# Another order within a step, a two-tile band, and the inner norm on one engine, in a two-layer banded kernel

## The chip, the cores and the metric

The kernel runs on one core of one Trainium2 chip. The metric is device time in microseconds (us), the median over runs. In the profile PE is TensorE's matmul queue and PEld its weight loads, DVE is VectorE, ACT is ScalarE, POOL is GpSimd and SP the engine that issues most DMAs.

## What is computed

x is [512, 512, 64] in float32. Two layers of the same form follow each other, x = x + f(gn(x)), where gn normalizes each pair of channels over the whole image. With m the mask product, L = 512, H = 128 and a window of 4, f is

```
xn    = ln(x)                                  # over the 64 channels
left  = (xn @ Wl + bl) * m * sigmoid(xn @ Wlg + blg)
right = (xn @ Wr + br) * m * sigmoid(xn @ Wrg + brg)
gate  = sigmoid(xn @ Wog + bog)
out[i, j, h] = sum over d in -4..4 of left[i + d, i, h] * right[i + d, j, h]
f     = (ln(out) * gate) @ Wo + bo
```

All is float32. Only a band of `left` is needed: row i + d of column i. For each h the sum over d is a small banded matrix (rows by rows) times the rows of `right`.

## The kernel before, in words

**Tiling.** `row_blocks` cuts the 512 rows into nine overlapping blocks of 64 rows (56 of them new, 60 at the ends). The image's left half of columns lies on partitions 0 to 63 and its right half on 64 to 127, e = 0 and 1. A block is two chunks of 128 columns a half, a chunk is 16 units (`NU`) of 8 columns (`JU`). So a layer has 18 chunks and 288 units. `layer` (line 748) runs steps t; a step carries one unit through projection and, 30 steps later (`LAG`), one `Out` through its end. The two layers run one after the other.

**A step**, for unit t and output t:

- `affine` and `inner_stats` prepare z of later units; `inner_norm` (437) and `inner_norm_v` (443) subtract the mean and scale, for the unit two steps ahead. GpSimd does six of eight columns in two instructions, VectorE the other two (`ZV`, 27) in two.
- `transposed` (450) turns z of the next unit on TensorE, `kept` (469) copies it from PSUM to `zT` on ScalarE, with a third part that repeats the first 64 columns, and stores it to `later` for the output's gates.
- `right` (514) projects the unit in two halves q = 0 and JQ = 4 through `crossed` (499): 8 matmuls a half, each with 64 rows, 128 columns of weights and 128 moving columns. `right_gate` (517) is the sigmoid on ScalarE, `right_end` (521) the product on VectorE into `RO`, a buffer that holds the right values of a chunk and later its outputs.
- `mix` (575) is the band: for 8 of the 128 h's it multiplies the banded left operand `A` with `RO`, 16 matmuls of 64 by 64 with 128 moving columns. The h's are split into two groups; the second group's results are written on the other half of the partitions (the "crossed" columns), so that all four 64x64 tiles of TensorE's array are used in turn. The result goes back from PSUM to `RO`, half by a ScalarE copy, half by a VectorE copy. A chunk has 16 mixes, spread over the first ten of 16 steps as 2, 1, 2, 2, 1, 2, 1, 2, 2, 1.
- `out_stats` (601) takes the statistics of `RO` on VectorE, `solve` (607) makes the scales every fourth step (a few small VectorE instructions, then a chain of small ones on GpSimd), `norm` (640) applies them on ScalarE into `on` (one buffer), 8 instructions a step in two groups of four.
- `gates` (653) and `gated` (666) make the output gate, `turned` (677) turns `on`, `times_gate` (690) multiplies both on VectorE into `ZH`. A step later `end` (713) multiplies by Wo, and `ended` (727) adds the residual, which `biased` (707) has prepared on GpSimd, and stores it. In layer 0 `sums` (736) collects the statistics for layer 1 on TensorE.

**The left operand.** In five early steps of a layer (3, 5, 7, 9, 11) `left` (528) projects the band of left into `L9`, a part of `RO`, and writes it to DRAM (`left_of`) when a row of nine is complete: 4 x 9 transfers a layer in pieces of 72 bytes. `take_left` (559) fetches 16 h's (`HA`) as `A` in four transfers with pieces of 512 bytes, [h, row, 2], into one of three buffers (`NA`).

**What sets the order.** Each engine runs its instructions in the order in which the program issues them (`InOrder`, 366, keeps the program's order). The order is that of the calls in lines 844 to 921, so moving a call moves its instructions on each engine's queue. PSUM has eight banks: `two_banks` (132) hands out two pairs in turn, to both right halves, the transposes and the mixes, in the order of the calls; each waits until the use two before it has been read. Four single banks go round among `gates`, `turned` and `end`.

Of the kernel before, what the change touches and what calls it, by code (L numbers as in the profile page):

```python
# [16 lines left out]
P = 128  # L17
# [9 lines left out]
ZV = 2  # L27
# [53 lines left out]
def tile_two_banded_layers(  # L81
# [28 lines left out]
    span = 2 * (S + 2 * WIN)  # L110
    size = S * H // 2 * span
# [325 lines left out]
    def inner_norm(u: Unit):  # L437
        n = ZV if u.at > NU else 0
        m = last(u.mean.rearrange("p k t -> p (k t)")[:, n:], D)
        en.gpsimd.tensor_tensor(u.z[:, n:], u.z[:, n:], m, ALU.subtract)  # L440
        en.gpsimd.tensor_tensor(u.z[:, n:], u.z[:, n:], last(u.rs[:, n:], D), ALU.mult)

    def inner_norm_v(u: Unit):
        for j in range(ZV if u.at > NU else 0):
            en.vector.tensor_scalar(
                u.z[:, j], u.z[:, j], u.mean[:, j // 2, j % 2 : j % 2 + 1], u.rs[:, j : j + 1],
                ALU.subtract, ALU.mult,
            )
# [20 lines left out]
    def kept(u: Unit):  # L469
        u.t = ztp.tile([P, JU // 2, P + S], F32, tag="zT", name="zT")  # L470
        to = u.t.rearrange("c k (n p) -> c n k p", n=3)
        for n, pt in enumerate(u.pt):
            en.scalar.activation(
                to[:, n : n + pt.shape[1]], pt.rearrange("c n (k p) -> c n k p", p=S),
                AF.Identity, bias=1.0,
            )
        if u.near is None:
            en.scalar.activation(
                to[:, 2], u.pt[0][:, 0].rearrange("c (k p) -> c k p", p=S), AF.Identity, bias=1.0
            )  # L480
            en.sync.dma_start(later[u.at], u.t[:, :, :P])
# [5 lines left out]
    def projected(u: Unit, q: int, w: bass.AP):  # L487

        pr = two_banks().rearrange("p (e k h) -> p e k h", e=2, k=JQ // 2)
        for k in range(JQ // 2):  # L490
            for e in range(2):
                part = slice(e * D, (e + 1) * D)
                en.tensor.matmul(
                    pr[:, e, k, :], lhsT=u.t[part, q // 2 + k, :P], rhs=w[part],
                    start=True, stop=True,
                )
        return pr

    def crossed(u: Unit, q: int, w: bass.AP):

        pr = two_banks().rearrange("p (e k h) -> p e k h", e=2, k=JQ // 2)
        for k in range(JQ // 2):
            for s in range(2):
                for e in range(2):
                    part = slice(e * D, (e + 1) * D)
                    en.tensor.matmul(
                        pr[:, e, k, :].rearrange("p (g s x) -> p g s x", g=2, s=2)[:, :, s],
                        lhsT=u.t[part, q // 2 + k, s * S : s * S + P],
                        rhs=w[part].rearrange("c (g s x) -> c g s x", g=2, s=2)[:, :, s],
                        start=True, stop=True,  # L510
                    )
        return pr

    def right(u: Unit, q: int, w: dict):
        u.pr[q] = crossed(u, q, w["right"]).rearrange("p e k h -> p (e k) h")
# [12 lines left out]
    def left(u: Unit, q: int, w: dict):  # L528
# [4 lines left out]
        sv = sg.rearrange("p (k e) h -> p e k h", e=2)  # L533
        for e in range(2):
            en.scalar.activation(sv[:, e], pr[:, e, :, H:], AF.Sigmoid)
        near = w["near"][:, n0 : n0 + JQ]
        en.gpsimd.tensor_tensor(sg, sg, last(near, H), ALU.mult)
        for e in range(2):
            en.vector.tensor_tensor(
                L9[:, :, n0 + e : n0 + JQ : 2, :],  # L540
                pr[:, e, :, :H].rearrange("p k (h t) -> p h k t", t=2),
                sv[:, e].rearrange("p k (h t) -> p h k t", t=2), ALU.mult,
            )
        for r in range(JQ):
            if n0 < (r + 1) * NEAR <= n0 + JQ:
                for n, b in enumerate(blocks):
                    q0 = b.s // JQ
                    at = n * size + r * (H // 2 * span + 2)
                    en.sync.dma_start(
                        strided(  # L550
                            left_of, at, (JQ * (H // 2 * span + 2), S // JQ), (span, H // 2),
                            (1, 2 * NEAR),
                        ),
                        L9[q0 : q0 + S // JQ, :, r * NEAR : (r + 1) * NEAR, :].rearrange(
                            "q h k t -> q h (k t)"
                        ),
                    )

    def take_left(n: int, h: int) -> bass.AP:


        A = lp.tile([P, HA // 2, S, 2], F32, tag="A", name="A")
        q = HA // 4
        for e in range(2):
            for s in range(2):
                en.sync.dma_start(
                    A[e * S : (e + 1) * S, s * q : (s + 1) * q].rearrange("p h i t -> p h (i t)"),
                    strided(
                        left_of, n * size + (s * H // 4 + h * q) * span + 2 * WIN,
                        (H // 2 * span, S), (span, q), (1, 2 * S),  # L570
                    ),
                )
        return A

    def mix(c: int, A: bass.AP, h0: int) -> list:


        j0 = c % 2 * (JC - JW)
        q = HB // 4
        R = RO.rearrange("p (s h) j t -> p s h j t", s=2)[:, :, h0 // 4 : h0 // 4 + q, j0 : j0 + JC]  # L580
        L = A.rearrange("p (s h) i t -> p s h i t", s=2)[:, :, h0 % HA // 4 : h0 % HA // 4 + q]
        pb = two_banks()
        ph = pb.rearrange("i (s h t j) -> i s h t j", s=2, h=q, t=2)
        for h in range(q):
            for t in range(2):
                for s in range(2):
                    for e in range(2):
                        part, to = (slice(n * S, (n + 1) * S) for n in (e, e ^ s))
                        en.tensor.matmul(
                            ph[to, s, h, t, :], lhsT=L[part, s, h, :, t], rhs=R[part, s, h, :, t],  # L590
                            start=True, stop=True,
                        )
        return [(R[:, s], ph[:, s].rearrange("i h t j -> i h j t")) for s in range(2)]

# [153 lines left out]
    def layer(src: bass.AP, dst: bass.AP, w: dict, stats: bool, then=None):  # L748
# [60 lines left out]
        for t in range(min(loads), last_t + 3):  # L809
# [34 lines left out]
            if t in lefts:  # L844
                for q in range(0, min(JU, NEAR * JQ - lefts[t].near), JQ):
                    left(lefts[t], q, w)
            if t in outs:
                gates(outs[t], w)
            if t in units:
                right(units[t], 0, w)  # L850
# [6 lines left out]
            if t in outs:  # L857
                gated(outs[t])
            if t in units:
                right_gate(units[t], 0)  # L860
            for v in looking[0:2]:
                out_stats(*v)
            for u in inputs(t + 2):
                inner_norm(u)
            for v in looking[2:5]:
                out_stats(*v)
            for v in todo:
                inner_stats(*v)
            if t in outs:
                turned(outs[t], w)  # L870
            for v in looking[5:]:
                out_stats(*v)
# [6 lines left out]
            if t in units:  # L879
                right_gate(units[t], JQ)  # L880
            if t in outs:
                biased(outs[t], w, stats)
            if t in units:
                right_end(units[t], 0)
# [173 lines left out]
```

## Time and profile before

| | |
|---|---|
| three runs, us | 4828.45, 4837.08, 4837.57; median 4837.08 |
| the profiled execution, us | 4837.08, of which its span 4835.3 |
| mean granted TensorE clock | 0.967 |
| ScalarE `on<-RO,nm,rs` 128x128 (`norm`) | 4608 of 499 ns mean, 1928.5 us busy |
| TensorE `banks<-pack,zT`, 128 columns (`right`) | 18432 of 285 ns mean, 1327.0 us busy |
| TensorE `banks<-RO,A` (`mix`) | 18432 of 281 ns mean, 632.2 us busy |
| VectorE `z<-z,sti,rs` (`inner_norm_v`) | 1084 of 647 ns mean, 657.1 us busy |
| GpSimd `z<-z,sti` and `z<-z,rs`, 128x384 (`inner_norm`) | 542 each, 842 and 838 ns mean |
| ScalarE `zT<-banks` 128x256 (the third part of zT) | 542 of 381 ns mean, 206.6 us busy |
| DMA, share of 16 engines' span | 73.0% on the first queue |

A float32 matmul stands as two instructions (a load and a matmul each), so a mix is 32. Instructions of one group overlap, and the busy time is the time in which at least one ran: it is less than count times mean. In the window lines below, the first numbers are the bounds of the window in us from the span's start and its length, then the busy time of each engine with its number of instructions. In the lines of waits the numbers are total us, how often, and the longest. Line 374 stands for all calls through `InOrder`, so groups are told apart by the names of their tiles: `banks` is a pair of PSUM banks, `bank` a single one.

### The profile page before, as it was taken

To read this page: it belongs to the slowest core of one execution; us is meant where nothing else is said; L and a number is where in the kernel's file an instruction comes from. 1 tells how busy PE (TensorE), PEld (TensorE's weight loads), DVE (VectorE), ACT (ScalarE), POOL (GpSimd) and SP (SyncE) were. 2 spreads that over 40 slices of the span, in tenths; PEclk is the share of its full clock that TensorE was granted. 3 is DMA by queue.
4 is the path that set the end of the run, shared out by engine and by line. 5 is a ranking of instruction groups with operands and counts; after the bars stand their busy time and mean duration, and the time that the engine had idled before them with its cause. 6 is when DMAs were issued, how large, how long until landed. Compare 5 with 4: busy or idle time off the path is not lost.

```text
span 4835.3 us, 193356 instructions
## 1 busy us (share of the span) xinstructions
PE 3858.8 (80%) x76306; PEld 3246.6 (67%) x76306; DVE 4360.2 (90%) x10719; ACT 3745.5 (77%) x8732; POOL 3599.2 (74%) x4739
## 2 busy tenths in 40 slices
PE   1025899999899998999974578888888888888898
PEld 0024677777777777777754467777777777777775
DVE  6954899999999999999966489999999999999997
ACT  0012798889889898889873278888888888888899
POOL 0035888888888888888634588888888888888863
PEclk9986999999999999999997799999999999999999
DMA  7858677777777777777764967777777777777776
GB/s 301 337 177 100 181 209 213 211 213 208 211 209 214 213 211 205 208 210 217 196 169 99 105 179 212 209 214 208 210 211 214 209 212 210 206 215 214 216 202 177
DMA packets 1437653, 983.61 MB, mean 203 GB/s; under 512 B 167202, under 2 KB 1284424, under 8 KB 1432392
## 3 DMA queue, kind: packets, MB, share of 16 engines
q1 hardware_dynamic: 1432064, 969.75, 73.0%
q8 instruction: 600, 9.83, 0.9%
q14 instruction: 309, 2.53, 0.2%
q10 hardware_dynamic: 4680, 1.50, 0.1%
HBM read 658.42 MB, written 312.46 MB: 201 GB/s over the span
## 4 chain that ended last, share of the span: by engine, by line
PE 39%; DVE 30%; DMA 11%; POOL 6%; issue 5%; ACT 5%; SPq 3%; ACTq 0%; DVEq 0%; POOLq 0%
PE banks L374 20%; PE bank L374 19%; DVE RO L374 8%; DVE z L374 6%; DVE ZH L374 5%; ACT on L374 3%; POOL z L374 3%; SPq L374 3%; DVE gn_st L374 3%; DVE sto L374 3%; DMA zg<-later 2%; DVE XR L374 2%; DVE sti L374 2%; DMA mid_x<-XR 1%; POOL rsqrt L374 1%
## 5 line engine op out<-in xcount | busy, mean ns | idle before, releaser
L374 ACT ACTIVATE on<-RO,nm,rs 128x128 f32<-128x128 f32 x4608 | 1928.5, 499 | 16.1 <-PE bank L374 12.7
L374 PEld LDWEIGHTS banks<-pack,zT 64*128 64x128 f32 x18576 | 1251.7, 195 | 562.5 <-DVE RO L374 304.7
L374 PE MATMUL banks<-pack,zT 64*128 64x128 f32 x18576 | 1359.7, 287 | 318.9 <-DVE RO L374 205.3
L374 DVE TENSOR_TENSOR RO<-banks,sg 128x512 f32<-128x512 f32 (+1 forms) x1188 | 753.1, 672 | 242.6 <-ACT sg L374 119.5
L374 ACT ACTIVATE sg<-banks 128x512 f32<-128x512 f32 (+1 forms) x1188 | 666.3, 594 | 280.4 <-PE banks L374 274.1
L374 DVE BATCH_NORM_STATS2 sto<-RO 128x6 f32<-128x256 f32 x2304 | 798.9, 408 | 1.2
L374 DVE SCALAR_TENSOR_TENSOR ZH<-bank,pack,gate 128x448 f32<-128x448 f32 (+1 forms) x1152 | 738.2, 682 | 63.2 <-ACT gate L374 49.8
L374 PE MATMUL bank<-zg,pack 64*128 64x448 f32 (+1 forms) x2304 | 724.9, 595 | 71.4 <-DMA zg<-later 43.4
L374 POOL TENSOR_TENSOR z<-z,gb 128x512 f32<-128x512 f32 x536 | 686.8, 1281 | 42.0
L374 POOL TENSOR_TENSOR z<-z,ga 128x512 f32<-128x512 f32 x536 | 684.7, 1277 | 6.8 <-DMA z<-in_x_dram 4.0
L374 PE MATMUL bank<-pack,ZH 128*64 128x64 f32 x18432 | 665.6, 225 | 5.6 <-ACT gate L374 5.1
L374 PE MATMUL banks<-RO,A 64*64 64x128 f32 x18432 | 632.2, 281 | 37.8 <-DVE RO L374 6.5
L374 DVE TENSOR_SCALAR z<-z,sti,rs 128x64 f32<-128x64 f32 x1084 | 657.1, 647 | 0.0
L374 PEld LDWEIGHTS bank<-pack,ZH 128*64 128x64 f32 x18432 | 585.8, 138 | 46.7 <-ACT gate L374 9.3
L374 PEld LDWEIGHTS banks<-RO,A 64*64 64x64 f32 x18432 | 531.4, 136 | 89.4 <-DVE RO L374 68.7
L374 ACT ACTIVATE zT<-banks 128x512 f32<-128x512 f32 (+1 forms) x1084 | 470.6, 488 | 134.4 <-PE banks L374 120.2
L374 ACT ACTIVATE gate<-bank 128x448 f32<-128x448 f32 (+1 forms) x1152 | 559.9, 539 | 13.0 <-issue 7.1
L374 POOL TENSOR_TENSOR z<-z,rs 128x384 f32<-128x384 f32 (+1 forms) x586 | 508.1, 867 | 45.9
L374 PE MATMUL bank<-ident,on 64*128 64x64 f32 x9216 | 473.6, 227 | 49.3 <-ACT gate L374 39.4
L374 POOL TENSOR_TENSOR z<-z,sti 128x384 f32<-128x384 f32 (+1 forms) x586 | 512.8, 875 | 0.0
L374 POOL TENSOR_TENSOR XR<-XR,pack 120x512 f32<-120x512 f32 (+1 forms) x352 | 417.2, 1188 | 121.3 <-DMA XR<-mid_x 51.5
L374 DVE BATCH_NORM_STATS2 sti<-z 128x6 f32<-128x128 f32 x2344 | 500.0, 278 | 0.7 <-DMA left_of<-RO 0.5
(145 smaller groups left out, 3981.4 us busy)
## 6 DMA issues: line engine op xcount, KB each, us to landing
later<-zT SPq DMA_DIRECT2D x576, 256.0 KB
A<-left_of SPq DMA_DIRECT2D x1152, 128.0 KB
zg<-later SPq DMA_DIRECT2D x576, 256.0 KB
z<-in_x_dram SPq DMA_DIRECT2D x576, 128.0 KB
z<-mid_x SPq DMA_DIRECT2D x576, 128.0 KB
gn_x<-in_x_dram SPq DMA_DIRECT2D x16, 4096.0 KB
XR<-in_x_dram SPq DMA_DIRECT2D x448, 112.0 KB
mid_x<-XR SPq DMA_DIRECT2D x448, 112.0 KB
```

What stands on the lines that cost most here:

```text
L374: return lambda *a, **k: tc.keep_in_program_order(f(*a, **k))
```

## The change

The title in a few words: the same work in another order within a step, and several pieces in another form.

- **Band.** `mix` uses two tiles: h's come in two turns of four; in a turn the upper half of the array works on four h's and the lower half on the other four, each writing to its own half of the partitions. `A` is now [row, 16 h], so that the stationary operand of an h is read at a step of 64 bytes. The copies back are of neighbouring h's.
- **Right.** `crossed` is gone; `right` uses `projected` (487), 4 matmuls a half with 256 moving columns. `zT` has no third part.
- **Left.** The left product stays in `sg`, ordered in slabs of 16 h's, and is written to `left_of` after each call, in pieces of up to 256 bytes. `take_left` fetches a slab in two transfers of 4 KB a row. `L9` is gone.
- **Inner norm.** GpSimd does all eight columns, `inner_norm_v` and `ZV` are gone.
- **Order.** The first right half and its gate, product and `inner_norm` come first, `gates` after the first half; `transposed`, `sums` and `end` come before the mixes; `then_affine` before `solve`; `biased` and the VectorE copies of the band are last.

```diff
     def inner_norm(u: Unit):
-        n = ZV if u.at > NU else 0
-        m = last(u.mean.rearrange("p k t -> p (k t)")[:, n:], D)
-        en.gpsimd.tensor_tensor(u.z[:, n:], u.z[:, n:], m, ALU.subtract)
-        en.gpsimd.tensor_tensor(u.z[:, n:], u.z[:, n:], last(u.rs[:, n:], D), ALU.mult)
+        z = u.z.rearrange("p (k t) c -> p k t c", t=2)
+        m = u.mean.unsqueeze(3).broadcast_to([P, JU // 2, 2, D])
+        en.gpsimd.tensor_tensor(z, z, m, ALU.subtract)
+        en.gpsimd.tensor_tensor(u.z, u.z, last(u.rs, D), ALU.mult)
...
     def kept(u: Unit):
-        u.t = ztp.tile([P, JU // 2, P + S], F32, tag="zT", name="zT")
+        u.t = ztp.tile([P, JU // 2, P], F32, tag="zT", name="zT")
...
-            en.scalar.activation(
-                to[:, 2], u.pt[0][:, 0].rearrange("c (k p) -> c k p", p=S), AF.Identity, bias=1.0
-            )
-            en.sync.dma_start(later[u.at], u.t[:, :, :P])
+            en.sync.dma_start(later[u.at], u.t)
...
-        u.pr[q] = crossed(u, q, w["right"]).rearrange("p e k h -> p (e k) h")
+        u.pr[q] = projected(u, q, w["right"]).rearrange("p e k h -> p (e k) h")
...
+        A = lp.tile([P, S, HA], F32, tag="A", name="A")
+        at = n * size + h * slab + WIN * HA
+        for e in range(2):
+            en.sync.dma_start(
+                A[e * S : (e + 1) * S].rearrange("p i h -> p (i h)"),
+                strided(left_of, at, ((S + 2 * WIN) * HA, S), (1, S * HA)),
+            )
...
+        R = RO[:, :, j0 : j0 + JC, :]
+        pb = two_banks()
+        ph = pb.rearrange("i (h j) -> i h j", j=JC)
+        for turn in range(2):
+            for h in range(HB // 2):
+                for e in range(2):
+                    part = slice(e * S, (e + 1) * S)
+                    hh = (turn ^ e) * (HB // 2) + h
+                    en.tensor.matmul(
+                        ph[part, hh, :], lhsT=A[part, :, h0 % HA + hh],
+                        rhs=R[part, (h0 + hh) // 2, :, hh % 2],
+                        start=True, stop=True,
+                    )
```

In `left` the writes are now

```diff
+        for o, r, k, m in runs(n0, n0 + JQ):
+            for n, b in enumerate(blocks):
...
+                en.sync.dma_start(
+                    strided(
+                        left_of, at, (JQ * (S + 2 * WIN + 1) * HA, S // JQ), (slab, H // HA),
+                        (1, m * HA),
+                    ),
+                    sl[q0 : q0 + S // JQ, :, o : o + m, :].rearrange("q s j x -> q s (j x)"),
+                )
```

The order of the calls of a step, before and after (without `left`, which is first in both):

```
before: gates(t), right 0, affine, right JQ, gated, right_gate 0, out_stats 0:2, inner_norm(t+2),
        out_stats 2:5, inner_stats, turned, out_stats 5:, solve, right_gate JQ, biased, right_end 0,
        right_end JQ, times_gate, norm(t+1) 0:4, end(t-1), inner_norm_v(t+2), then_affine, sums(t-2),
        transposed(t+1), mix 0, kept(t+1), ScalarE copy 0, mix 1, ScalarE copy 1, ended(t-1),
        VectorE copy 0, norm(t+1) 4:8, VectorE copy 1
after:  right 0, gates(t), out_stats 0:2, right_gate 0, inner_norm(t+2), right_end 0, gated, affine,
        right JQ, out_stats 2:5, turned, transposed(t+1), then_affine, sums(t-2), out_stats 5:,
        end(t-1), right_gate JQ, norm(t+1) 0:4, kept(t+1), right_end JQ, inner_stats, mix 0, solve,
        times_gate, mix 1, norm(t+1) 4:8, ScalarE copy 0, ScalarE copy 1, ended(t-1),
        VectorE copy 0, biased(t), VectorE copy 1
```

`solve` runs in every fourth step; `then_affine` is the affine of the next step, taken ahead in those steps. `later`, `zg`, `XR` and z transfers are issued by SP in the same order as before, except that the store of `later` moves with `kept`.

## The prediction, made before the changed kernel ran

> **What bounds the kernel now.** I read the busy totals first, then windows in the steady part of each layer, then single steps, then the waits.
>
> ```profile
> PE 3858.8 (80%) x76306; PEld 3246.6 (67%) x76306; DVE 4360.2 (90%) x10719; ACT 3745.5 (77%) x8732; POOL 3599.2 (74%) x4739
> ```
>
> ```profile
> 652.00:2393.00 1741.00, 1589.16 (x33605) 1372.67 (x33600) 1689.76 (x4117) 1554.65 (x3601) 1480.89 (x1910) 1.00 0.76 211
> 2948.00:4681.00 1733.00, 1510.72 (x29769) 1260.15 (x29770) 1692.66 (x4118) 1536.30 (x3602) 1479.68 (x1910) 0.99 0.76 211
> ```
>
> The two windows are 15 chunks (240 steps) of layer 0 and of layer 1: length, then busy time of PE, PEld, DVE, ACT and POOL, then clock, DMA share and GB/s. Divided by 240, a step lasts 7.25 us in layer 0 and 7.22 in layer 1. VectorE is busy 7.04 and 7.05 of that (97%), TensorE 6.62 and 6.29, ScalarE 6.48 and 6.40, GpSimd 6.17 in both. So VectorE is the bound on average, with 0.2 us a step lost beside it. But the average hides three kinds of steps: of 16 steps in a chunk six have no band mix, four have one, six have two (the list `step` in `layer`).
>
> ```profile
> 1108.59:1114.25 5.66, 5.66 (x109) 5.04 (x109) 5.38 (x15) 5.66 (x14) 5.01 (x11) 1.00 0.90 245
> 1134.24:1140.67 6.43, 6.43 (x144) 5.49 (x140) 6.31 (x16) 6.28 (x15) 5.94 (x10) 1.00 0.84 231
> 1140.67:1156.87 16.20, 15.02 (x349) 13.00 (x345) 15.94 (x38) 14.06 (x33) 15.81 (x15) 1.00 0.72 203
> ```
>
> Same columns: one step of layer 0 without a mix, one with one, and two in a row with two each. In the first TensorE and ScalarE are both full. In the second TensorE alone is full. In the third VectorE fills 15.94 of 16.20 and TensorE 15.02: it waits about 0.6 us a step. The waits say for what:
>
> ```profile
> PEld banks L374 <- DVE RO L374: 574.6, 760, 2.7
> POOL rsqrt L374 <- DVE rs L374: 462.9, 141, 29.8
> PE banks L374 <- DVE RO L374: 378.3, 446, 3.0
> ```
>
> TensorE waits for VectorE to empty PSUM pairs (band copies and right products).
>
> **The change, part by part.**
>
> *Band on two tiles instead of four.*
>
> ```profile
> 1083.99 2.03 PE L374 MATMUL banks<-pack,zT 64*128 64x128 f32 x32
> ...
> 1088.49 1.14 PE L374 MATMUL banks<-RO,A 64*64 64x128 f32 x32
> ```
>
> ```profile
> 1147.16 2.19 PE L374 MATMUL banks<-RO,A 64*64 64x128 f32 x64
> ```
>
> Start, length, instructions (the first two in a one-mix step, the third in a two-mix step); those of 128 columns count here. The projection works on two tiles at a time: 32 instructions are 16 rounds of two. Less the last instruction's own 0.28 us (the group's mean is 281 ns), (2.03 - 0.28)/15 = 0.117 us a round. The band works on four: a mix of 32 is 8 rounds, (1.14 - 0.28)/7 = 0.123 us, and two mixes are 16 rounds, (2.19 - 0.28)/15 = 0.127. So a round costs 0.12 us whether two or four instructions lie in it. The new `mix` still issues 32 instructions, but only the two diagonal tiles are used: 16 rounds, 1.9 us instead of 0.95. That is +0.95 us of TensorE a mix. There are 18432/32 = 576 mixes and 576 unit steps, so +0.95 us a step on average, 547 us in all, none of it optional.
>
> *Stationary operand of the band 64 bytes apart* (A becomes [row, 16 h], before [h, row, 2], 8 bytes apart). The trace shows no load at that step: 64 columns 8 bytes apart load in 136 ns, contiguous ones (`bank<-pack,ZH`) in 138 ns, 128 contiguous ones (`banks<-pack,zT`) in 195 ns. The longer load sits under the projection's 0.117 us rounds without lengthening them. Bounds: 0, the nearest row (8 bytes cost nothing against contiguous); and two rounds for one, +1.9 us a mix, if a load at that step were twice the longest load seen and no longer fitted. Below nothing is excluded, since loads are hidden already. I take 0, and keep the other end as a rival.
> [...]
>
> *Right projection uncrossed.* 8 instructions a half of 256 columns instead of 16 of 128, the same columns. The left projection has that form: at 322.91, in the slow-clock start, its 16 instructions take 3.79 us, and 32 of 128 columns take 3.39 at 333.83. Bounds +0.4 us a step by that pair and -0.2 (half the loads, one change of tile shape fewer in a step); I take 0.
>
> *Two of eight inner norms back on GpSimd.* VectorE loses two instructions a step, whose price depends on GpSimd:
>
> ```profile
> 1140.31 2.08 DVE L374 TENSOR_SCALAR z<-z,sti,rs 128x64 f32<-128x64 f32 x2
> ...
> 1147.97 0.61 DVE L374 TENSOR_SCALAR z<-z,sti,rs 128x64 f32<-128x64 f32 x2
> ```
>
> ```profile
> 448.30 1.05 POOL L374 TENSOR_TENSOR z<-z,sti 128x512 f32<-128x512 f32 x1
> ...
> 457.28 0.84 POOL L374 TENSOR_TENSOR z<-z,sti 128x384 f32<-128x384 f32 x1
> ```
>
> The pair takes 0.61 us or, beside GpSimd's own norm, 2.08. In all it is 657.1 us busy, 1.14 a step. VectorE falls to 7.04 - 1.14 = 5.9. GpSimd's two norms grow from 0.84 to 1.05 each, +0.42 a step: 6.17 becomes 6.6. With the group's mean (1.28, mostly startup) it would be +0.87, 7.05. I take 1.05: at 440 to 450 us, with no VectorE work on z beside it, each of these instructions takes 1.04 or 1.05; the mean holds ones at 1.50 too.
>
> *zT without its third part.* ScalarE loses the 128x256 copy, 206.6 us busy, 0.36 a step: 6.1 is left. TensorE stays full in the steps without a mix, so little of that shows there.
>
> *Left operand in slabs.* A comes in 576 transfers of 4 KB rows instead of 1152 of 512-byte rows. SP saves about 576 x 0.615 us of issue (`A<-left_of`, median), beside the rest. That can remove at most the waits for `zg<-later` (43.4 + 25.9 us); I take 0, as these steps wait for banks next. On the way out, 12 runs x 9 blocks = 108 transfers a layer replace 36, from `sg`, which has two buffers that the right gates share. So a right gate now waits for transfers to land, with `kept` queued behind it. Before, those same steps wait for `later<-zT` behind the left issues (90.6 us in all). Bounds: -90 and +40 (108 x 0.6 against 36 x 1.24 us, two layers); I take 0.
>
> *The order.* Band copies end VectorE's step; two of them are 1.3 us, and the first right half and the gates on TensorE (0.95 + 0.85 us) now lie between the last mix and the second half that needs the freed pair: covered. If that cover went, it would cost up to 1.3 us in a two-mix step. The transposes and `kept` move ahead of the band, so a mix no longer waits for `kept`. `then_affine` moves ahead of `solve` on GpSimd. Every fourth step GpSimd then runs norm 2.1, two to three affines at 2.55 each, and only then the ten rsqrt steps and two products (about 3.6): the scale for ScalarE's `norm` of the next step is ready 11 to 14 us after the step began. Queued behind `norm` on ScalarE are `kept` and the band copies, for which TensorE waits. Before, that slot was an idle wait of GpSimd for VectorE (462.9 us above).
>
> **The sum.** By kind of step in layer 0: without a mix TensorE stays near 5.6; with one 6.43 + 0.95 = 7.4; with two 6.43 + 3 x 0.95 = 9.3, against about 8.1 now. (6 x 5.6 + 4 x 7.4 + 6 x 9.3)/16 = 7.44. Layer 1 lacks the sums into `acc` (0.57 us): 5.5 (ScalarE), 6.8 and 8.7, that is 7.03. I add the 0.2 us that a step loses now and 0.05 for late rsqrt: 7.69 and 7.28, or +0.44 and +0.06 against 7.25 and 7.22. Times 288 steps each: +144 us. The profiled execution took 4837.08 us (span 4835.3 and 1.8 around it) and is itself the median of the three. 4837 + 144, with a few us off for the start: **4975 us**, its own range 4870 to 5080.
>
> **Rivals.**
> *VectorE's relief wins (faster).* Place: the two-mix steps. If the lost 0.2 us a step disappears, because TensorE no longer waits for VectorE, and steps without a mix drop to 5.3, the averages are 7.3 and 6.95: +0.05 and -0.27, times 288 = -63 us, 4774; a tenth of the good ends of the DMA and start terms (-69, -90) makes 4760, all of them 4615. It decides if a two-mix step stays under about 8.9 us. For it: 953 us of bank waits on VectorE (both TensorE queues, in part the same time). Against: TensorE is full in the other ten steps already.
> *GpSimd becomes the bound.* Norms at 1.28 us, 7.05 us busy a step, rsqrt late by 3 us in two of every four solves: +0.35 a step more than the forecast's on half of the steps, 5080 us. For it: 15.81 of 16.20 us busy in the two-mix window. Against: the 1.05 row.
> *The 64-byte loads show.* Rounds double: 576 x 1.9 = +1094, less what hides; half of it gives 5520 us. Against: 8 bytes cost nothing.
>
> **How the numbers follow.** Forecast 0.52, GpSimd 0.14, loads 0.10, VectorE's relief 0.20, nothing in sum 0.04. The range runs from 4770 to 5240: it leaves out half of the relief case and most of the loads case. A measurement here tells some 0.2% from no change, so faster 0.20, same 0.04, slower 0.76.
>
> **What would show it.** Band groups of 32 at about 1.9 to 2.1 us with no wait inside; VectorE near 82% in the steady windows and TensorE above 95%; `z<-z,sti` 128x512 at 1.05; two-mix steps near 9.3 us in layer 0. Wrong if the band's rounds are longer than 0.13 us, if GpSimd is fuller than TensorE, or if two-mix steps stay near 8.1.

## The result, and the profile after

The changed kernel takes 4875.28 us (median of 4 runs, 4872.71 to 4880.72), the kernel before 4837.32 on the same chip: ratio 1.0082, 95% interval 1.0064 to 1.0099. It is slower by 0.8% (+38 us), where +2.85% (+138) was forecast. On another chip before took 4871 and the changed kernel 4878 (ratio 1.0016, 1.0005 to 1.0027). The kernel before took 4837 to 4839 us in two of six comparisons, and 4869 to 4871 in the other four; the changed kernel ran in two of them and hardly differs. Why is open, so a ratio below is always to before on the same chip.

The profiled execution took 4876.42 us, of which its span 4874.6. Its totals:

```profile
PE 4107.5 (84%) x67090; PEld 3507.8 (72%) x67090; DVE 3830.6 (79%) x9635; ACT 3642.8 (75%) x8156; POOL 3804.8 (78%) x4739
```

VectorE gives up 530 us, TensorE gets 249 more, and the bound moves from the one to the other. The windows of 15 chunks in each layer, with the columns of those shown for before:

```profile
662.00:2406.00 1744.00, 1682.89 (x29762) 1486.47 (x29760) 1450.22 (x3637) 1511.03 (x3361) 1573.76 (x1907) 1.00 0.74 210
2976.00:4717.00 1741.00, 1601.24 (x25922) 1369.20 (x25920) 1468.72 (x3636) 1497.48 (x3361) 1574.47 (x1907) 0.99 0.74 210
```

Divided by 240: steps of 7.27 and 7.25 us (before 7.25 and 7.22), TensorE 7.01 and 6.67 (96% and 92%), VectorE 6.04 and 6.12, GpSimd 6.56 in both. So an average step is nearly as long as before, with another engine full. Of the 39.3 us that the span grew, 6.2 lie ahead of the first output step, 6.6 in layer 0, 12.6 in the change of layers and 13.9 in layer 1.

Steps of the changed kernel in the same view: without a mix, with one, two in a row with two each (all layer 0), and one of layer 1 that is told of below:

```profile
1102.05:1107.64 5.59, 5.07 (x95) 4.28 (x93) 4.83 (x13) 4.92 (x12) 5.43 (x6) 1.00 0.69 196
1029.52:1036.56 7.04, 7.04 (x127) 6.20 (x125) 5.86 (x14) 6.26 (x14) 6.61 (x10) 1.00 0.89 244
1036.56:1054.30 17.74, 17.74 (x315) 16.06 (x313) 13.89 (x34) 14.01 (x31) 17.27 (x15) 1.00 0.71 207
3375.16:3385.21 10.05, 8.82 (x143) 7.53 (x141) 9.36 (x25) 7.91 (x18) 8.72 (x18) 1.00 0.59 171
```

With one and with two mixes TensorE is full to the last hundredth: 7.04 and 8.87 us a step, where the forecast had 7.4 and 9.3. Of the waits that it names, TensorE's for VectorE are mostly gone, GpSimd's for `rs` is not, and TensorE now waits for ScalarE's `zT`:

```profile
DVE RO L373 <- ACT RO L373: 427.7, 495, 2.4
POOL rsqrt L373 <- DVE rs L373: 401.6, 154, 34.3
PEld banks L373 <- ACT zT L373: 343.0, 254, 11.4
PE banks L373 <- ACT zT L373: 294.0, 241, 11.3
PEld banks L373 <- DVE RO L373: 175.0, 365, 1.5
PE banks L373 <- DVE RO L373: 49.7, 101, 2.2
```

TensorE's two queues waited 953 us for VectorE before, and 225 now (in part the same time on both queues). For `zT` they waited 271 us before, and 637 now. The groups that the steps of the prediction touch (count, then busy us and mean ns, then idle time before):

```profile
L373 PE MATMUL banks<-pack,zT 64*128 64x256 f32 x9360 | 1335.1, 407 | 358.1 <-ACT zT L373 281.3
...
L373 PE MATMUL banks<-RO,A 64*64 64x128 f32 x18432 | 1154.5, 277 | 19.9 <-ACT zT L373 12.7
L373 PEld LDWEIGHTS banks<-RO,A 64*64 64x64 f32 x18432 | 1082.5, 183 | 46.9 <-ACT zT L373 15.2
...
L373 POOL TENSOR_TENSOR z<-z,sti 128x512 f32<-128x512 f32 x586 | 620.8, 1059 | 0.0
```

The band is busy 1154.5 us against 632.2, and its loads take 183 ns against 136. GpSimd's norm is at 1059 ns, as forecast.

### The profile page after: what moved, and what is told of

Read it like the earlier page. It is cut to its first block, busy times and chain, and to the rows that moved or that the text cites. A ratio compares the mean times of both kernels' runs of the same rounds, so it can differ in the third digit from the quotient of the medians.

```text
span 4874.6 us, 173394 instructions
## 1 busy us (share of the span) xinstructions
PE 4107.5 (84%) x67090; PEld 3507.8 (72%) x67090; DVE 3830.6 (79%) x9635; ACT 3642.8 (75%) x8156; POOL 3804.8 (78%) x4739
## 4 chain that ended last, share of the span: by engine, by line
PE 56%; DVE 15%; ACT 12%; POOL 6%; DMA 4%; issue 3%; SPq 3%; ACTq 0%; POOLq 0%; DVEq 0%
PE banks L373 36%; PE bank L373 18%; ACT on L373 6%; DVE gn_st L373 3%; POOL rsqrt L373 3%; DVE RO L373 3%; SPq L373 3%; PE acc L373 3%; DVE sto L373 3%; ACT gate L373 2%; ACT zT L373 2%; DVE sti L373 2%; DVE ZH L373 2%; ACT sg L373 1%; DVE var L373 1%
## 5 line engine op out<-in xcount | busy, mean ns | idle before, releaser
L373 PE MATMUL banks<-pack,zT 64*128 64x256 f32 x9360 | 1335.1, 407 | 358.1 <-ACT zT L373 281.3
L373 PEld LDWEIGHTS banks<-pack,zT 64*128 64x128 f32 x9360 | 893.5, 195 | 731.7 <-ACT zT L373 327.8
L373 PE MATMUL banks<-RO,A 64*64 64x128 f32 x18432 | 1154.5, 277 | 19.9 <-ACT zT L373 12.7
L373 PEld LDWEIGHTS banks<-RO,A 64*64 64x64 f32 x18432 | 1082.5, 183 | 46.9 <-ACT zT L373 15.2
L373 DVE TENSOR_TENSOR RO<-banks,sg 128x512 f32<-128x512 f32 x1152 | 788.2, 684 | 396.3 <-ACT sg L373 376.4
L373 DVE COPY RO<-banks 128x512 f32<-128x512 f32 x576 | 397.8, 691 | 430.0 <-ACT RO L373 427.7
L373 POOL TENSOR_TENSOR z<-z,rs 128x512 f32<-128x512 f32 x586 | 613.1, 1046 | 46.0
L373 POOL TENSOR_TENSOR z<-z,sti 128x512 f32<-128x512 f32 x586 | 620.8, 1059 | 0.0
L373 ACT COPY RO<-banks 128x512 f32<-128x512 f32 x576 | 335.1, 582 | 284.3 <-PE banks L373 280.0
L373 PEld LDWEIGHTS bank<-ident,on 64*128 64x128 f32 x9216 | 404.9, 139 | 125.7 <-ACT gate L373 36.7
```

Source lines behind the costliest of these rows:

```text
L373: return lambda *a, **k: tc.keep_in_program_order(f(*a, **k))
```

## The experiments

The change has three parts that can be had apart: the **forms** (two-tile band, plain right projection, slabs, short zT), the **norm** (all on GpSimd) and the **order**. My theory after the result: the forms and the norm cost and bring what the sum says, and the error lies in the order, which was taken at nothing. Rivals: the band's cost was too high, the norm's gain too low, or what is lost beside the bound is another wait than I thought (the 64-byte loads, or late scales, through `then_affine` or without it). The texts on record before each run say what each expects; where they number theories, 2 is `then_affine`, 3 the place of ScalarE's band copies, and 4 is VectorE: its load where it is a theory, and late scales in another way where it is a rival to 2. They name kernels by short labels: e5_norm is the norm alone, e2_forms the forms alone, e1_order_norm order and norm, and e4_affine_late the changed kernel with `then_affine` behind `solve`.

| forms | norm | order | us | ratio to before |
|---|---|---|---|---|
| – | – | – | 4871 | 1 |
| – | yes | – | 4812 | 0.9878 (0.9863 to 0.9893) |
| yes | – | – | 5102 | 1.0471 (1.0452 to 1.0489) |
| – | – | yes | 5234 | 1.0745 (1.0722 to 1.0768) |
| yes | yes | – | 5011 | 1.0286 (1.0268 to 1.0303) |
| yes | – | yes | 5084 | 1.0433 (1.0418 to 1.0449) |
| – | yes | yes | 4960 | 1.0176 (1.0158 to 1.0194) |
| yes | yes | yes | 4878 | 1.0016 (1.0005 to 1.0027) |

### One part each

The norm alone:

```diff
-ZV = 2
+ZV = 0
```

> The kernel before with all of the inner norm on GpSimd, nothing else changed. Theory 4 (VectorE, 97% busy, is the bound before, and the norm's return is what makes the changed kernel cheap): VectorE falls from 7.05 to 5.9 us a step, GpSimd rises to 6.6, TensorE has 6.3 and 5.85 without waits, ScalarE 6.4; a step takes 6.8 to 7.0 and the ratio to before is 0.95 to 0.98. Rival 5 (before's waits lie in the order, not in VectorE's load): 0.99 to 1.01.

4812 us: this one line beats before by 1.2% and the changed kernel by 1.3%. The ratio lies between the two ranges that were expected, as VectorE's relief brings less than theory 4 had. The forms alone, in the old order and with the norm split:

```diff
-    pr[:, e, k, :].rearrange(...)[:, :, s], lhsT=u.t[part, q // 2 + k, s * S : s * S + P],
+    pr[:, e, k, :], lhsT=u.t[part, q // 2 + k, :], rhs=w[part],
...
-    for s in range(2):
-        for e in range(2):
-            part, to = (slice(n * S, (n + 1) * S) for n in (e, e ^ s))
+    for e in range(2):
+        part = slice(e * S, (e + 1) * S)
+        hh = (turn ^ e) * (HB // 2) + h
```

> The changed kernel with the order of before and two of eight inner norms on VectorE as before: the forms (two-tile band, plain right projection, slabs) alone. Theory 1 (forms cost, order and norm give it back): TensorE's unstalled time is 6.3 - 0.1 + 0.95 = 7.15 us a step in layer 0 and 6.7 in layer 1, VectorE stays at 7.0 and the two still wait for each other, so 7.6 to 8.0 a step, 5040 to 5270 us. Rival 2 (the forms are hidden under VectorE, and the order is what lost the 0.8%): 4820 to 4860 us.

5102 us, +4.7%. The order alone, as listed under "after" in the section on the change, with the band copies last:

> The kernel before with only the order changed; the norm stays split, its two VectorE instructions stand ahead of inner_stats. Theory 6 (the new order needs VectorE's slack and the long two-tile band; alone it adds waits for the band's PSUM pairs and GpSimd's lock on VectorE's norm): ratio 1.03 to 1.06. Rival 6 (the order is neutral): 0.99 to 1.01.

5234 us, +7.5%, more than both ranges: in the old forms the order is far from neutral, and bad. (The granted clock in this profile is 0.96 and 0.93 in the windows of 662 to 2406 and 2976 to 4717 us, where the changed kernel has 1.00 and 0.99; how much of the 7.5% goes with that is not shown. What the text calls GpSimd's lock is in the trace of before this: of VectorE's 1084 `z<-z,sti,rs` all 646 that took over 0.34 us, up to 1.37, ended 0.05 us after an instruction of GpSimd. What it adds in this kernel is not shown either.)

### Two parts each

All three pairs: order and norm with the old forms, the changed kernel with VectorE's two norms put back ahead of `inner_stats`, and forms and norm in the old order.

> The kernel before with the order of the changed kernel and all of the inner norm on GpSimd; band on four tiles, crossed right projection, third part of zT and left path stay as before. Theory 1 (the changed kernel is held by TensorE, 7.0 of 7.27 us a step in layer 0, and the two-tile band is 0.93 us a mix of that): TensorE falls to about 6.1, the next bounds are GpSimd 6.6 and ScalarE 6.4 to 6.7, a step takes 6.8 to 7.0, so 4640 to 4730 us, clearly faster than both. Rival 1 (GpSimd, 91% busy and late with the scales, is the real bound of the changed kernel): a step stays at 7.2, 4830 to 4880 us.

> The changed kernel with two of eight inner norms on VectorE as before, placed ahead of inner_stats. Theory 4 (the norm's return relieves the bound): VectorE goes from 6.05 to 7.2 us a step and waits come back, ratio to before 1.02 to 1.05, near e2_forms. Theory 1 (TensorE alone holds the changed kernel, VectorE has 1.2 us to spare): within 0.5% of the changed kernel. Rival 1 (GpSimd holds it): faster than the changed kernel, ratio below 1.00.

> The changed kernel with the order of before: forms and norm together, no reordering. Theory 5 (TensorE alone holds it, and the new order saves TensorE about 0.1 us of unstalled time a step by its neighbours, and hides the band's return): groups of the band 2.03 us, gates back to 0.86 and turned to 0.6 us, a step of layer 0 at 7.3 to 7.5, ratio to before 1.01 to 1.03. Rival 6 (the order does nothing for the two-tile band either): within 0.3% of the changed kernel, 1.00 to 1.005.

4960, 5084 and 5011 us. The first is slower than both of its ranges, so neither of the two bounds that they name explains it. The other two lie where theories 4 and 5 had them. Beside them ran the changed kernel, so that it stands beside before on such a chip:

> The changed kernel as it is, beside the others on the same chip: all theories expect 1.00 to 1.01, and about the time of e4_affine_late.

4878 us. So, with the two other parts in place, the forms are worth -1.6% (4960 to 4878), the norm -4.1% (5084 to 4878) and the order -2.7% (5011 to 4878, 133 us), while alone they are +4.7, -1.2 and +7.5%. No part has a price of its own.

Forms and norm in the old order is the kernel that the forecast's sum described: +140 us, where it had +144. (It ran on a chip where before takes 4871; on the chip of the result, where before takes 4837, it did not run.) A one-mix step of it in layer 0, from TensorE's timeline:

```profile
1111.41 1.02 PE L374 MATMUL bank<-zg,pack 64*128 64x448 f32 x4
1112.26 1.89 PE L374 MATMUL banks<-pack,zT 64*128 64x256 f32 x16
1113.99 0.89 PE L374 MATMUL bank<-ident,on 64*128 64x64 f32 x16
1114.81 1.15 PE L374 MATMUL bank<-pack,ZH 128*64 128x64 f32 x32
1115.79 0.64 PE L374 MATMUL acc<-XR 120*64 120x65 f32 x16
1116.36 0.46 PE L374 MATMUL banks<-ident,z 64*128 64x64 f32 x8
1116.75 2.10 PE L374 MATMUL banks<-RO,A 64*64 64x128 f32 x32
1118.79 1.02 PE L374 MATMUL bank<-zg,pack 64*128 64x448 f32 x4
```

A line is start, length, engine and group; an idle time ahead of it would stand in brackets. From `gates` to `gates` it lasts 7.38 us. The median of such steps in layer 0 is 7.4, without a mix 5.7, and those with two take 9.2 to 10.1: the forecast's 5.6, 7.4 and 9.3, with waits in the last. The same step of the changed kernel:

```profile
1029.53 1.13 PE L373 MATMUL banks<-pack,zT 64*128 64x256 f32 x7
1030.49 0.92 PE L373 MATMUL bank<-zg,pack 64*128 64x448 f32 x4
1031.24 1.03 PE L373 MATMUL banks<-pack,zT 64*128 64x256 f32 x8
1032.10 0.69 PE L373 MATMUL bank<-ident,on 64*128 64x64 f32 x16
1032.60 0.44 PE L373 MATMUL banks<-ident,z 64*128 64x64 f32 x8
1032.97 0.69 PE L373 MATMUL acc<-XR 120*64 120x65 f32 x16
1033.49 1.10 PE L373 MATMUL bank<-pack,ZH 128*64 128x64 f32 x32
1034.52 2.11 PE L373 MATMUL banks<-RO,A 64*64 64x128 f32 x32
1036.56 1.13 PE L373 MATMUL banks<-pack,zT 64*128 64x256 f32 x8
```

It lasts 7.03 us, with the same work. Read by differences of starts, projection and gates take 2.58 us in the old order and 2.57 in the new, and the band 2.04 in both. All of the difference lies between `turned` and the mix: 2.76 us against 2.42.

One part that the lines show is `gated`. In layer 0 three single banks go round (the fourth, told of in the section on the kernel, is `acc` there). `gates` takes two, `turned` two and `end` one, so `turned` and `end` need the banks of the gates back. In the old order ScalarE comes to `gated` behind `norm` 4:8, at 1113.59 in that step, 0.4 us before `turned` begins, and its second half ends at 1114.54. In 15 chunks of layer 0 TensorE's loads wait 35.3 us for `gate` in that kernel, 150 times, and 0.7 us, twice, in the changed one.

A two-mix step of layer 0 gains more, 9.49 to 8.89 us on average. There the transposes of the old order also wait for the pair that `right_end 0` gives back, the longest in the step that ends at 1111.41:

```profile
1107.03 0.46 PE L374 MATMUL banks<-ident,z 64*128 64x64 f32 x8 [0.69 <-DVE RO L374]
```

Steps without a mix lose: 5.67 to 5.80 us in layer 0 and 5.32 to 6.08 in layer 1. In both orders `kept` stands behind `norm` 0:4 on ScalarE, but the new one begins a step with `right 0`, which needs `zT`, where the old one has `gates` first: in 15 chunks of each layer TensorE's loads wait 73.5 and 118.5 us for `zT`, where they waited 4.7 and 15.1.

### Where the new order loses with the four-tile band

> e1_order_norm (four-tile band and the other forms of before, order of the changed kernel, norm on GpSimd) with both copies of each mix directly behind it on ScalarE and VectorE, ahead of norm 4:8, times_gate or ended. Theory 3 (e1 waits because the band's PSUM pair is freed late: ScalarE's copy stands behind norm 4:8, VectorE's copy starts only after ScalarE's, and a four-tile band is too short to cover that; 0.7 to 1.5 us in each step with a mix): these waits go, a step takes 6.7 to 7.0, ratio 0.94 to 0.97. Rival 1 (GpSimd or its late scales are the bound): ratio stays at 1.01 to 1.02.

In the kernel with order and norm, the copies of a mix were put directly behind it on both engines, and `norm` 4:8 behind them. It took 4974 us (1.0219, 1.0202 to 1.0235), against 4960. The view behind the idea is right, from TensorE's, then ScalarE's, then VectorE's timeline of order and norm:

```profile
1046.86 2.06 PE L373 MATMUL banks<-RO,A 64*64 64x128 f32 x64
1050.40 1.16 PE L373 MATMUL banks<-pack,zT 64*128 64x128 f32 x16 [1.48 <-DVE RO L373]
```

```profile
1047.47 1.68 ACT L373 ACTIVATE on<-RO,nm,rs 128x128 f32<-128x128 f32 x4
1049.05 1.05 ACT L373 COPY RO<-banks 128x512 f32<-128x512 f32 x2
```

```profile
1049.66 1.29 DVE L373 COPY RO<-banks 128x512 f32<-128x512 f32 x2 [0.43 <-ACT RO L373]
```

The two four-tile mixes end at 1048.9. ScalarE is in `norm` 4:8 until 1049.05, VectorE's copies start only as ScalarE's of the same pair ends, and the projection waits 1.48 us for the pair. (That VectorE's copy comes second is the program's doing: in the trace each of the 576 has one wait, for a semaphore that ScalarE's copy raises, though the two copy different banks of the pair. In the changed kernel that makes 427.7 us of waits. No run lets them go side by side.) With the two-tile band the mixes take 3.9 us instead of 2.06, and `norm` 4:8 lies beside them. As far as the lines show, that is what the long band buys, and why the forms are a gain in this order. But with the copies first, two-mix steps of layer 0 fell from a median of 9.4 to 8.3 us and one-mix steps rose from 6.1 to 7.8, as the copies now stand ahead of `times_gate` and the norm: the place of the wait (3) was right, the cure was not.

### The rivals about loads and late scales

The changed kernel, with the band's stationary operand read contiguously:

```diff
+        AC = A.rearrange("p i h -> p (i h)").rearrange("p (h i) -> p h i", h=HA)
...
-                        ph[part, hh, :], lhsT=A[part, :, h0 % HA + hh],
+                        ph[part, hh, :], lhsT=AC[part, h0 % HA + hh, :],
```

> The changed kernel with the stationary operand of the band read from 64 neighbouring elements of the same slab instead of elements 64 bytes apart. The values multiplied are others, so the output is not the reference's; the work is the same. Theory 1 (loads at 64 bytes take 183 ns instead of 136, as long as a load of 128 columns, and hide under the 0.12 us rounds): loads fall to about 136 ns, the band's groups stay at 2.03 us a mix, time within 0.2% of the changed kernel. Rival 3 (the strided loads hold the rounds up): the band's groups get shorter than 1.9 us a mix, and 0.1 us x 576 = 58 us or more goes away, 4820 us or less.

4863 us (0.9983, 0.9973 to 0.9993), 0.3% under the changed kernel. Its load group:

```profile
L373 PEld LDWEIGHTS banks<-RO,A 64*64 64x64 f32 x18432 | 1033.0, 131 | 46.9 <-ACT zT L373 15.5 <-DVE RO L373 9.3
```

A load is 131 ns instead of 183. The loads do show, by 15 us of 4878, a little more than the 0.2% of theory 1 and far less than rival 3 had. Then the affines behind `solve`, in the changed kernel, and ahead of it, in the kernel with the norm alone (the three lines that the diff moves are the loop over `then_affine`):

> The changed kernel with the affine taken ahead (then_affine) put back behind solve on GpSimd. Theory 2 (in layer 1 the steps after two of four solves are 1.5 and 3.1 us long because GpSimd does two to three affines before the scales): these steps fall back to 8.5 and 5.6, 4.6 us a chunk x 18 = 83 us in layer 1 and 1 us a chunk in layer 0, so 4780 to 4830 us. Rival 4 (the scales are late because VectorE delivers the statistics late, and GpSimd then idles and has the affine left over): no gain or a loss, 4870 to 4930 us.

> e5_norm with the affine taken ahead (then_affine) moved ahead of solve on GpSimd, as in the changed kernel. Theory 2b (GpSimd is 92% busy in e5_norm and idles at solve until VectorE delivers; the affine fills that): 0.975 to 0.985. Rival 4 (the scales get later by one affine, 2.5 us in every fourth step): 0.99 to 1.00.

The first took 4872 us (1.0002, 0.9990 to 1.0014, not told apart from the changed kernel's 1.0016), the second 4858 (0.9974, 0.9964 to 0.9985, against 0.9878). So in the old order `then_affine` ahead of `solve` costs 1%, and in the new one next to nothing: there GpSimd waits for VectorE's `rs` anyway (401.6 us, 154 times, where in the kernel with the norm alone it is 223.7 us, 87 times). In layer 1 one step in 16 lasts 10.05 us and another 8.0 (medians) instead of 8.6 and 5.6; putting the affines back leaves them at 10.1 and 7.6. So the theory that `then_affine` makes the scales late (2) fell for this kernel, and its rival (4) stands, that VectorE's own part comes late. VectorE and GpSimd in the changed kernel at the first:

```profile
3374.03 1.22 DVE L373 TENSOR_SCALAR var<-var 128x32 f32<-128x32 f32 x1
...
3375.29 0.20 DVE L373 TENSOR_SCALAR rs<-var 128x64 int32<-128x64 int32 x1
```

```profile
3375.56 0.29 POOL L373 TENSOR_TENSOR rsqrt<-rs 128x64 f32<-128x64 f32 x1 [0.35 <-DVE rs L373]
...
3379.87 0.25 POOL L373 TENSOR_TENSOR nm<-nm,rs 128x32 f32<-128x32 f32 x1
```

VectorE's part comes behind `inner_stats`, one of its instructions takes 1.22 us (with the affines behind `solve` too), and GpSimd's chain is 4.6 us long; ScalarE's `norm`, with `kept` and the copies behind it, waits until 3380.15. The last kernel of this group leaves one norm of eight on VectorE (`ZV = 1` in the kernel with the norm alone):

> The kernel before with one of eight inner norms on VectorE instead of two (e5_norm has none). Theory 4 (VectorE's load): VectorE at 6.5 us, GpSimd at 6.4, TensorE 6.3, all even: 0.98 to 0.99, like e5_norm or a little under it. Rival 5: 1.00.

4815 us (0.9885, 0.9866 to 0.9904), the same as with none.

### Which part of the order does it

If TensorE's own sequence makes the 133 us, it must work in the old order too. Into forms and norm went first `transposed` and `sums` ahead of `end`, then `gates` behind the first half as well, all on TensorE alone:

```diff
+            for u in inputs(t + 1):
+                transposed(u)
+            if stats and t - 2 in outs:
+                sums(outs[t - 2], t - 2 == first_t, t - 2 == last_t)
             if t - 1 in outs:
                 end(outs[t - 1], w)
```

> The order of before with the changed forms and the norm on GpSimd (5011 us where before takes 4871), with one edit: on TensorE the transposes of z and the sums stand between `turned` and `end`, where `end` stood directly behind `turned`. Nothing moves on another engine. Theory A (the order's 133 us are TensorE's neighbours: in the old order `end` waits behind `turned` for the gates' bank to be read, 781 against 492 ns, and `sums` takes 568 against 515): 0.29 to 0.34 us less in each of 576 steps at most, and some of it lost to other waits: 4850 to 4920 us. Theory B (the gain is in the other engines' order, above all right_end ahead of the rest and the band copies last): 5000 to 5020 us, no change.

> The same, and the output gates behind the first half of the projection: TensorE's order is now that of the changed kernel, all other engines' order that of before. Theory A: 4860 to 4900 us, the changed kernel's 4878 or close to it, as the gates' place adds 0.1 us a step (855 against 751 ns) to the neighbours' part. Theory B: 5000 to 5020. A third one (each engine's order is worth something only with the others'): 4920 to 4980.

5456 us (1.1212, 1.1191 to 1.1232) and 5513 (1.1320, 1.1299 to 1.1341). None of the expectations held: 9 to 10% slower than the old order. The other way round, the changed kernel with `turned`, `end`, `sums`, `transposed` in the old sequence:

> The changed kernel with one edit undone: on TensorE `turned` is followed by `end`, `sums` and the transposes, as before the change. Theory A: 0.2 to 0.3 us more a step, 4980 to 5040 us. Theory B: 4870 to 4890, no change.

4911 us (1.0091, 1.0077 to 1.0105), between the two ranges: 33 us, a quarter of the 133.

```profile
1033.19 0.69 PE L373 MATMUL bank<-ident,on 64*128 64x64 f32 x16
1033.81 1.15 PE L373 MATMUL bank<-pack,ZH 128*64 128x64 f32 x32
...
1035.75 3.95 PE L373 MATMUL banks<-RO,A 64*64 64x128 f32 x64
```

From `turned` to the mix it takes 2.56 us against 2.42, without a wait: 0.14 us are the groups' neighbours alone. The other 0.20 of the 0.34 above go with the rest of the order, and they lie in `turned`: from its start to that of `end` it takes 0.82 us in the old order and 0.62 here, with the same neighbours. `turned` and `transposed` have one shape of tile (64*128 in the lines), `sums` and `end` others, so the old sequence has a change of shape more. Layer 0's step grows from 7.27 to 7.42 us; layer 1's stays at 7.26, though the same stretch grows by 0.14 us there too (1.92 to 2.06 in a one-mix step). That the change of shape is what costs the 0.14 us is not shown: no run here changes the shape alone.

TensorE's order in the kernel with the norm alone and the four-tile band:

> The kernel before with the inner norm on GpSimd alone (4812 us where before takes 4871), four-tile band and crossed projection kept, with TensorE's order of the changed kernel and all other engines' order of before. Theory A: there the transposes are at half the width of the gates' tiles too, so the neighbours save up to 0.2 us a step, but TensorE isn't alone the bound: 4720 to 4810 us. Its rival (the order needs the long band to cover the return of the banks, as the order with the four-tile band took 4960): 4900 to 4960 us, slower.

5057 us (1.0389, 1.0373 to 1.0404): slower as well. In both kernels the transposes, now early, wait for the pair of the first half, which `right_end 0` gives back: TensorE's matmuls wait 611 us for `RO` on VectorE with the neighbours moved, 133 in the old order of the same kernel, and 660 against 271 with the four-tile band. So `right_end 0` was put behind `inner_norm`, in each:

```diff
             for u in inputs(t + 2):
                 inner_norm(u)
+            if t in units:
+                right_end(units[t], 0)
```

> The kernel of the second run above (TensorE's order of the changed kernel, all other engines in the old order, 5513 us) with one edit: `right_end 0` on VectorE stands directly behind `inner_norm`, ahead of the later statistics and of `solve`, as in the changed kernel, so that the pair of banks of the first half comes back before the transposes ask for it. Theory C (TensorE's order is worth something only once the pair it takes earlier is also given back earlier): most of the loss goes, 4880 to 5010 us, at or under the 5011 of the old order. Rival: the pair is held by ScalarE's part (right_gate JQ, `kept`, the copies), and this edit gives back less than half: 5250 to 5500.

> The same edit in the kernel with the four-tile band, the crossed projection, the norm on GpSimd and TensorE's order of the changed kernel (5057 us). Theory C: it falls under the 4812 of the same kernel in the old order, 4740 to 4810 us. Rival: 4900 to 5050, as the short band leaves less time for the return of the pairs.

5590 us (1.1553, 1.1537 to 1.1569) and 5217 (1.0777, 1.0761 to 1.0792): worse again. ScalarE in the first of them, a two-mix step and the next:

```profile
1111.23 0.59 ACT L374 COPY RO<-banks 128x512 f32<-128x512 f32 x1 [1.25 <-PE banks L374]
1111.71 1.67 ACT L374 ACTIVATE on<-RO,nm,rs 128x128 f32<-128x128 f32 x4
1113.28 0.96 ACT L374 ACTIVATE gate<-bank 128x448 f32<-128x448 f32 x2
1114.13 1.08 ACT L374 ACTIVATE sg<-banks 128x512 f32<-128x512 f32 x2
```

and in the changed kernel:

```profile
1045.55 0.58 ACT L373 COPY RO<-banks 128x512 f32<-128x512 f32 x1 [1.25 <-PE banks L373]
1046.61 0.60 ACT L373 ACTIVATE sg<-banks 128x512 f32<-128x512 f32 x1 [0.47 <-PE banks L373]
```

In the old order of ScalarE the right gate `sg` comes 2.9 us after the band copy starts, behind `norm` 4:8 and `gated`; in the new one 1.06 us after, as soon as the first half is there. With `right_end 0` early, VectorE, which runs in order, stands still for it:

```profile
DVE RO L374 <- ACT sg L374: 284.3, 267, 6.7
```

```profile
DVE RO L374 <- ACT sg L374: 900.5, 568, 8.5
```

(without and with the early `right_end 0`). So TensorE's sequence alone costs time, with VectorE's early product it costs more, and only the whole order gains. That it is ScalarE's order that was missing in the last two kernels is read from these lines; no run puts it in alone, and both took longer than the rival had.

## Why the prediction was right and wrong, step by step

- **What bounds.** Right: TensorE became the bound, at 96% in layer 0; VectorE fell to 83 and 84% of the steady windows (82% said). In layer 1 TensorE has 92%, where above 95% was said.
- **Band, +0.95 us a mix.** Right: a group of 32 takes 2.03 us with one mix, 3.87 with two, where it took 1.08 and 1.99: +0.95 and +0.94 each.
- **64-byte loads, 0.** Nearly: a load takes 183 ns at 64 bytes, 136 at the 8 of before and 131 contiguous, and most of that lies under the rounds: read contiguously, the same loads make the kernel 15 us shorter.
- **Right projection, taken at 0 between +0.4 and -0.2.** The two rows behind the +0.4 stand at different granted clocks, the 3.79 us at 0.50 and the 3.39 at 0.57. The -0.2 was an estimate of mine that rests on no row: before doesn't show if a change of tile shape costs anything. All of `banks<-pack,zT` is busy 1335.1 us, where it was 1327.0 and, at 256 columns, 33.2: 25 us less in 576 steps.
- **Norm.** Right in its prices: 1.06 us an instruction, GpSimd 6.56 us a step (6.6 said), VectorE 6.04 to 6.12 (5.9 said). The rival with GpSimd as the bound is out: TensorE is fuller. One reading of the prediction is loose: of the pair that took 2.08 us, the second instruction lay beside GpSimd's `biased`, not its norm, and the pair of 0.61 began beside the norm.
- **The order, "covered", taken at 0.** This is the step that failed. With forms and norm in place the order is worth -133 us (5011 to 4878). The miss is 137 us where these kernels ran (+144 summed, +7 measured) and 106 on the chip of the result (+38 measured). The term that it hits is TensorE's own time. In 240 steps of each layer without the order TensorE is busy 7.43 and 7.03 us a step, where the sum has 7.44 and 7.03; with the order it is busy 7.01 and 6.67. The working asked only whether the late copies were covered, and priced every group of TensorE as it stood in the old order. It didn't ask what TensorE's groups cost beside other neighbours (33 us, shown by one run), nor what the earlier right gate, product and `gated` would free (the other 100 us, which no run splits further; the lines show the wait for the gates' banks in `turned`, and in two-mix steps that of the transposes for their pair).
- **The 0.2 + 0.05 us lost beside the bound.** Wrong by layer. Without the order, layer 0's step is 7.53 us and layer 1's 7.46, where 7.69 and 7.28 were forecast: 0.10 and 0.44 us are lost beside TensorE, where 0.25 was put in each. The two errors cancel, by luck, which is why the sum without the order fits (+140 and +144 us). With the order the steps are 7.27 and 7.25, and 0.26 and 0.58 are lost. So layer 1's forecast is met by luck too, a TensorE that is 0.36 us cheaper and 0.33 more lost, and on the chip of the result the miss lies in layer 0: 0.42 us in each of 288 steps, 121 us (the start and the change of layers take 19 of it back). Layer 1's loss is late scales, as said, but not through `then_affine`.
- **Start and SP, a few us off.** The start costs 6 us more and the change of layers 13, both small. The right gates do wait for the slabs' transfers, 103.2 us in all; the waits for `later` that they replace were 90.6, so the 0 nearly held.
- **The kinds of steps.** Without a mix 5.6 (median of layer 0; 5.8 on average), right; with one 7.03 for 7.4, with two 8.87 for 9.3. "It decides if a two-mix step stays under about 8.9" was the rival's condition for a gain. It was met, by 0.03, but steps without a mix didn't drop to 5.3, so norm and order together made up for most of the band and brought no gain.

The small difference hides large terms: the forms alone cost 4.7% (4871 to 5102 us), then the norm gives back 1.8 (to 5011) and the order 2.7 (to 4878). Taken in another sequence the parts have other sizes.

## What to carry to other kernels

A new order has a price of its own: price each group of the bounding engine beside its new neighbours, and follow each buffer round its whole loop (who frees it, and what is queued ahead of that on each engine), before calling a move covered. Parts that were tuned together are tested together and one by one: here every part alone has another sign or size than in company. And the one-line part, the norm on GpSimd alone, was the best kernel of all (4812 us; 4815 with one of eight left on VectorE is the same).

## What the runs showed of the hardware

- A VectorE instruction on 128x32, `var<-var`, took 1.15 to 1.23 us 18 of the 144 times it ran in the changed kernel; the other 126 took 0.18 to 0.2. Each of the 18 lay beside GpSimd's `z<-z,gb` and ended 0.04 us after it, the one shown at 3375.25.
- A float32 load of 64 columns for the band took 131 ns contiguous, 136 at a step of 8 bytes and 183 at 64, under rounds of 0.12 us.
